# Layer 1's third step: operands kept in SBUF, the bias added by TensorE, VectorE's order tied, the second step's last product first

## The chip, the cores and the metric

The kernel runs on one core of a Trainium2 chip. The metric is the device time of one execution in microseconds (us), from the runs listed below. A profile of one execution gives the time of each instruction on each engine: TensorE (PE), VectorE (DVE), ScalarE (ACT), GpSimd (POOL) and SyncE (SP), whose queue here issues loads. Matrices that a matmul produces lie in PSUM, in banks of 512 fp32 columns; everything else that an engine works on lies in SBUF, and the large arrays in device memory (HBM).

## The reference

Four graph layers run one after the other on 16 graphs of 1024 nodes with 128 features. Each layer's result is added to its input and normalised row by row. The change is in layer 1, which makes three steps of the following kind on an adjacency that was thinned out first; each step's batch normalisation needs the statistics of all 16 graphs.

```python
def _sage(x, adj, Wr, Wx, b, mf):
    deg = jnp.clip(jnp.sum(adj, axis=-1, keepdims=True), 1.0, None)
    agg = jnp.einsum('bij,bjd->bid', adj, x) / deg
    out = agg @ Wr + x @ Wx + b
    nrm = jnp.maximum(jnp.linalg.norm(out, axis=-1, keepdims=True), NORM_EPS)
    return out / nrm * mf[..., None]
...
h1 = _bn(jax.nn.relu(_sage(x, adj_d, Wr1, Wx1, b1, mf)), g1, be1)
h2 = _bn(jax.nn.relu(_sage(h1, adj_d, Wr2, Wx2, b2, mf)), g2, be2)
h3 = _bn(jax.nn.relu(_sage(h2, adj_d, Wr3, Wx3, b3, mf)), g3, be3)
xc = jnp.concatenate([h1, h2, h3], axis=-1) * mf[..., None]
return (xc @ Wl + bl) * mf[..., None]
```

## The kernel before

`fast_kernel` does the work; a general version behind it runs only where a flag says that the inputs are not of the expected kind, which they are here. `B` is 16 graphs (called batches), `N` 1024 nodes, `P` 128 partitions, `NT` 8 blocks of 128 nodes, `H2` two halves of 512 columns.

The thinned adjacency lies in SBUF as `Y[b]`, 8 KB of each partition for a batch, in tiles named `carry_...`. Before layer 1 the tiles of batches 0 to 7 are written to HBM (`dil8_d`) and given up; batches 8 to 15 stay. Every step takes the batches in the order 8 to 15, then 0 to 7.

A step is an object of class `Step`, with `l` 0, 1 or 2. Its parts are generators that `take_turns` runs a piece at a time, so that the code of several batches is interleaved:

- `load(b)` fetches the operands. In step three (`l == 2`) these are `hT` (the batch's features, turned) and `ag` (its aggregation), 512 KB each, from `hT_d[1]` and `ag_d`, by SP's queue.
- `out(b)` multiplies, for each of 8 blocks, `hT` by `Wx` and `ag` by `Wr` (L1410, fp32, two passes of TensorE each) into a PSUM bank for four blocks. VectorE adds the bias row and writes `o` (L1412). ScalarE squares `o` into the bank (L1418), VectorE sums the squares (L1419). Then `power_mhalf` takes the floor on VectorE (L744) and the power -1/2 on GpSimd (L745), VectorE multiplies by the mask (L1422) and makes `n`, the rectified and normalised rows (L1426).
- `keep(b)` turns `n` by eight transposes on TensorE (L759), ScalarE copies them to `nT` (L1435), VectorE takes the statistics of the batch normalisation (L1436), and GpSimd's queue stores `nT` (L1437). In steps one and two it goes on: `n` is split in two parts, the adjacency is widened to fp32 pieces `a`, TensorE multiplies (L1306, 32 matmuls of two passes over the two parts in all, each pass 512 columns), VectorE divides by the degree (L1445) and GpSimd's queue stores `ag` (L1447). That product is what the next step loads.

The normalisation of a step is not applied to its rows. `norm` turns the statistics into a scale and a shift (L1340 to L1345), and `take_norm` puts them into the next step's `Wr` and `Wx` and, by a small matmul `pc` (L1333), into its bias row `brow` (L1334). So step three's weights need all of step two's statistics. The last batch of step two is the exception in the order: its statistics come first (`next(rest)`), and the rest of its `keep`, in the list `left`, is interleaved with the first round of step three.

The order on each engine is not that of the program text: the framework places instructions by estimated times, within what the data and buffers allow. A buffer that is used again waits for its last readers. In PSUM there are four banks of tag `h` (`ps_h`), which `out` and the transposes share, and four of tag `acc` (`ps_a`), which the products of the adjacency use. In SBUF, `nT` of step three has two buffers, `n`, `ag` and `hT` three each.

During step three the memory of layer 2 is opened (`Layers23`), its weights are loaded and scaled (L1207 to L1232, two transposes at L709 and L838), and the inputs of its first batches are loaded (`hb`, `A`, `xn`, L1244 to L1251). Layer 2's first matmuls (`py`, L1568) multiply `hb` by `Wl`; `hb` has one buffer for each of the three steps' results.

Of the kernel before, what the change touches and what calls it, by code (L numbers as in the profile page):

```python
# [22 lines left out]
P = 128  # L23
# [616 lines left out]
def fast_kernel(ctx: ExitStack, tc: tile.TileContext, t: dict, out: bass.AP, flag: bass.AP):  # L640
# [46 lines left out]
    def nat(ap):  # L687
        return ap.rearrange("(t p) d -> p t d", p=P)
# [569 lines left out]
    with ExitStack() as ph:  # L1258
# [39 lines left out]
        def adjacency_product(pieces, parts):  # L1298

            for h in range(H2):  # L1300
# [6 lines left out]
                                             start=(jt == 0 and p == 0), stop=(jt == NT - 1 and p == 1))  # L1307
                yield acc, slice(h * 512, (h + 1) * 512)

        class Step:  # L1310


# [14 lines left out]
            def take_norm(self):  # L1327

                ab = bn_ab[self.l - 1]
                ws = wts.tile([P, P], F32, name="ws")  # L1330
                nc.vector.tensor_add(ws, self.Wr, self.Wx)
                pc = ps_h.tile([P, P], F32, name="pc", tag="h")
                nc.tensor.matmul(pc, ab[:, 1:2].to_broadcast([P, P]), ws, start=True, stop=True)  # L1333
                nc.vector.tensor_add(self.brow, self.brow, pc)  # L1334
                nc.vector.tensor_scalar(self.Wr, self.Wr, ab[:, 0:1], None, op0=OP.mult)
                nc.vector.tensor_scalar(self.Wx, self.Wx, ab[:, 0:1], None, op0=OP.mult)

            def norm(self):
                mv = wts.tile([P, 2], F32, name=f"bmv{self.l}")
# [7 lines left out]
            def load(self, b):  # L1347
# [6 lines left out]
                if self.l == 0:  # L1354
                    st.x = work.tile([P, NT, P], F32, name="n", bufs=3)
                    nc.sync.dma_start(st.x, nat(x1_d[b]))
                else:

                    tag, bufs = ("rdeg", 3) if self.l == 2 else ("hT", 2)
# [41 lines left out]
            def out(self, b):  # L1401

                st = self.batches[b]
                o = work.tile([P, NT, P], F32, name="o", tag="oT")
                banks = []
                for p, _, blocks in halves(ps_h):
                    banks.append(tiles3(p))
                    for i, j in enumerate(blocks):
                        for n, (x, W) in enumerate(((st.hT, self.Wx), (st.ag, self.Wr))):
                            nc.tensor.matmul(p[:, i * P:(i + 1) * P], x[:, j * P:(j + 1) * P], W,  # L1410
                                             start=(n == 0), stop=(n == 1))
                    nc.vector.tensor_add(o[:, blocks[0]:blocks[-1] + 1, :], tiles3(p),  # L1412
                                         self.brow[:, None, :].to_broadcast([P, 4, P]))
                yield
                ss = small.tile([P, NT], F32, name="ss")
                for h, sq in enumerate(banks):
                    k = slice(4 * h, 4 * h + 4)
                    nc.scalar.activation(sq, o[:, k, :], AF.Square)  # L1418
                    nc.vector.tensor_reduce(ss[:, k], sq, AX.X, OP.add)  # L1419
                yield  # L1420
                rn = power_mhalf(small, ss, floor=1e-24, name="rn")
                nc.vector.tensor_mul(rn, rn, mf[:, b * NT:(b + 1) * NT])  # L1422
                st.n = work.tile([P, NT, P], F32, name="n", bufs=3)
                for h in range(H2):
                    k = slice(4 * h, 4 * h + 4)
                    nc.vector.scalar_tensor_tensor(st.n[:, k, :], o[:, k, :], 0.0, half_rows(rn[:, k]),  # L1426
                                                   op0=OP.max, op1=OP.mult)
                yield

            def keep(self, b):  # L1430

                st = self.batches[b]
                nT = work.tile([P, N], F32, name="nT", tag="hi" if self.l == 2 else "oT")
                for p, c, k in turned(ps_h, st.n):
                    nc.scalar.copy(nT[:, c], p)  # L1435
                    nc.vector.bn_stats(self.stats[:, b * H2 + k.start // 4, :], nT[:, c])  # L1436
                nc.gpsimd.dma_start(hT_d[self.l][b], nT)  # L1437
                yield
                if self.l < 2:
                    parts = split(st.n)  # L1440
                    pieces = list(widened(st.A))
                    yield
                    ag = work.tile([P, N], F32, name="ag", bufs=3)
                    for acc, c in adjacency_product(pieces, parts):
                        nc.vector.tensor_mul(ag[:, c], acc, st.rdeg[:, c])  # L1445
                        yield
                    nc.gpsimd.dma_start(ag_d[b], ag)  # L1447
                yield

        before = None  # L1450
# [5 lines left out]
        for l in range(3):  # L1456
            step = Step(l, before)
            if l:
                before.norm()
                step.take_norm()  # L1460
            lead = 0 if l == 1 else 1
            take_turns([step.load(b) for b in order[:1 + lead]])
            if l == 0:
# [2 lines left out]
            for i in range(B + lag[l]):  # L1466
# [2 lines left out]
                    streams.append(step.load(order[i + 1 + lead]))  # L1469
                if l == 0 and i + 1 < B:  # L1470
                    streams.append(step.first(order[i + 1]))
                if i < B:
                    streams.append(outs[i] if l < 2 else islice(outs[i], 1))
                if l == 2 and i:
                    streams.append(outs[i - 1])
                if i > lag[l]:
                    streams.append(step.keep(order[i - 1 - lag[l]]))
                take_turns(streams)
                if l == 2 and i == 0:

# [273 lines left out]
```

## Time and profile before

| what | time |
|---|---|
| median of 3 runs | 2961.86 us |
| lowest and highest run | 2958.01 and 2962.2 us |
| the profiled execution | 2964.0 us |
| its span, first to last instruction | 2962.2 us |
| TensorE busy in the span | 2725.4 us (92%) |
| VectorE busy | 2196.2 us (74%) |
| ScalarE busy | 2024.2 us (68%) |
| GpSimd busy | 325.8 us (11%) |

In the views that follow, a line of a group gives the line of the program, the engine, the operation, the output and input tiles, the shapes and the count; then the busy time in us and the mean of one in ns; then the idle time of the engine just before, with what ended it. In the table by stage each engine has its busy time in us and its count of instructions; `PEclk` is the granted clock of TensorE as a share of the full one, and the DMA share is that of the core's 16 DMA engines. The chain of waits is followed back from the end: each piece has its start, its length and what it was. The timeline has start, length, engine and instruction.

### The profile page before, as it was taken

The page shows a single profiled execution, that of the slowest core. Times are in us where ns is not written, and L with a number is a line of the kernel's source. Part 1 is how long each engine was busy: PE and PEld are TensorE (multiplying, and loading weights), DVE is VectorE, ACT ScalarE, POOL GpSimd, SP SyncE. Part 2 cuts the span into 40 slices and gives each one's busy share as a digit, 9 for nine tenths or more (in the row PEclk, how much of TensorE's full clock was granted, in tenths as well). Part 3 has the DMA queues.
Part 4 walks back from the last instruction along what each step waited for, and adds up shares of the span by engine and source line. Part 5 has one row for each costly group of instructions (what it writes and reads, how often), then busy time and mean ns, then how long its engine had stood idle before and what let it go on. Part 6 is the DMA issues. An engine that isn't in the chain of part 4 may idle for free.

```text
span 2962.2 us, 42088 instructions
## 1 busy us (share of the span) xinstructions
PE 2725.4 (92%) x14771; PEld 1695.2 (57%) x14834; DVE 2196.2 (74%) x6087; ACT 2024.2 (68%) x3476; POOL 325.8 (11%) x295
## 2 busy tenths in 40 slices
PE   7999999996999889999899988999999999999996
PEld 3444444443666657877788873555555555555554
DVE  5777777777999976776688785777777777776765
ACT  6788888874788786666555435666666667676753
POOL 0000000030000001111122230001000101000000
PEclk9999999997999999999999997999999999999998
DMA  5444444420000052233467681111111111111000
GB/s 187 135 157 151 163 163 157 151 91 16 2 2 2 2 195 82 100 107 136 162 212 266 228 327 50 47 62 64 61 68 69 60 58 57 57 57 57 22 15 23
DMA packets 124125, 297.91 MB, mean 101 GB/s; under 512 B 12672, under 2 KB 65664, under 8 KB 116736
## 3 DMA queue, kind: packets, MB, share of 16 engines
q1 hardware_dynamic: 103440, 211.65, 21.6%
q0 software_dynamic: 20464, 83.47, 7.1%
q8 instruction: 119, 1.95, 0.3%
q14 instruction: 102, 0.84, 0.1%
HBM read 211.04 MB, written 84.02 MB: 100 GB/s over the span
## 4 chain that ended last, share of the span: by engine, by line
PE 36%; issue 19%; DVE 17%; POOL 4%; ACT 4%; DMA 2%; SPq 0%; POOLq 0%; DVEq 0%; ACTq 0%
PE ph L1550 8%; PE acc L1306 7%; PE ph L766 5%; PE acc L1626 4%; PE ph L1410 3%; PE pmm L724 3%; POOL ln_rstd L745 2%; PE ph L759 2%; DVE ln_st L794 2%; PE ph L1536 2%; DVE em L1612 2%; ACT xn L801 2%; POOL rn L745 1%; DVE A L1679 1%; PE acc L981 1%
## 5 line engine op out<-in xcount | busy, mean ns | idle before, releaser
L724 PE MATMUL pmm<-G,hT 128*128 128x512 f32 x1024 | 512.8, 614 | 10.7 <-DVE mx L1612 6.7
L801 ACT ACTIVATE xn<-xn,ln_nb,ln_rstd 128x128 f32<-128x128 f32 x512 | 207.4, 481 | 112.9 <-DVE ln_nb L799 112.8
L724 PEld LDWEIGHTS pmm<-G,hT 128*128 128x128 f32 x1024 | 175.0, 193 | 166.7 <-issue 118.3
L745 POOL TENSOR_TENSOR ln_rstd<-ln_rstd,mhalf 128x8 f32<-128x8 f32 (+1 forms) x68 | 115.9, 1704 | 1323.9 <-DVE nmx L1614 606.7
L1306 PE MATMUL acc<-a,lo 128*128 128x512 f32 x768 | 243.5, 401 | 15.5 <-DVE lo L1273 15.5
L1626 PE MATMUL acc<-em,hs 128*128 128x512 f32 x512 | 251.8, 611 | 3.5 <-DVE hs L1623 1.9
L981 PE MATMUL acc<-em,hs 128*128 128x512 f32 x512 | 245.7, 601 | 6.5 <-DVE hs L978 5.6
L1306 PE MATMUL acc<-a,hi 128*128 128x512 f32 x768 | 244.1, 402 | 3.7 <-ACT hi L1272 3.5
L1145 ACT ACTIVATE q<-s,negc 128x512 f16<-128x512 f32 x256 | 170.6, 697 | 59.2 <-DVE negc L1124 22.3
L1143 PE MATMUL s<-step,carry 128*128 128x384 bf16 (+3 forms) x1034 | 199.4, 304 | 7.9 <-DVE carry L1113 3.2
L1157 ACT ACTIVATE carry<-pc,negone 128x512 fp8e4<-128x512 f32 x256 | 166.8, 699 | 38.3 <-PE pc L1156 28.9
L972 DVE CUSTOM_DVE_ANT_0 em<-pmm,msk 128x1024 f32<-128x1024 f32 x128 | 155.9, 1218 | 40.6 <-PE acc L981 20.3
L1306 PEld LDWEIGHTS acc<-a,lo 128*128 128x128 f32 x768 | 144.4, 190 | 54.8 <-DVE lo L1273 21.1
L1612 DVE CUSTOM_DVE_ANT_0 em<-pmm,msk 128x1024 f32<-128x1024 f32 x128 | 155.6, 1216 | 25.9 <-PE acc L1626 21.3
L922 ACT ACTIVATE carry<-an 128x1024 fp8e4<-128x1024 f32 x128 | 134.4, 1050 | 50.7 <-DMA an<-in_adj 50.5
L1306 PEld LDWEIGHTS acc<-a,hi 128*128 128x128 f32 x768 | 143.0, 190 | 37.1 <-ACT hi L1272 4.0
L1607 ACT ACTIVATE msk<-A,nbig 128x1024 bf16<-128x1024 fp8e4 x128 | 145.9, 1140 | 26.6 <-DVE mx L1612 23.4
L974 ACT ACTIVATE em<-em,mx 128x1024 f32<-128x1024 f32 x128 | 146.0, 1141 | 25.4 <-DVE mx L972 22.7
L981 PEld LDWEIGHTS acc<-em,hs 128*128 128x128 f32 x512 | 90.9, 189 | 123.9 <-issue 87.2
L1410 PE MATMUL ph<-Wx,hT 128*128 128x128 f32 x768 | 153.4, 282 | 3.0 <-ACT nT L1435 1.4
L1410 PE MATMUL ph<-Wr,ag 128*128 128x128 f32 x768 | 151.1, 279 | 1.4 <-DMA ag<-ag_d 1.2
L1666 ACT CAST A<-A 128x1024 fp32r<-128x1024 fp8e4 x64 | 64.2, 1040 | 124.8 <-PE ph L1550 124.6
(294 smaller groups left out, 6181.9 us busy)
## 6 DMA issues: line engine op xcount, KB each, us to landing
an<-in_adj SPq DMA_DIRECT2D x128, 512.0 KB, 3.5
adj_d<-carry POOLq DMA_DIRECT2D x16, 1024.0 KB, 4.2
A<-dil_d SPq DMA_DIRECT2D x16, 1024.0 KB, 7.1
rdeg<-rdeg_d SPq DMA_DIRECT2D x32, 512.0 KB, 4.2
ag_d<-ag POOLq DMA_DIRECT2D x32, 512.0 KB, 5.3
ag<-ag_d SPq DMA_DIRECT2D x32, 512.0 KB, 6.3
A<-adj_d SPq DMA_DIRECT2D x16, 1024.0 KB, 4.7
xn<-in_x SPq DMA_DIRECT2D x16, 512.0 KB, 4.2
```

The costliest lines, as they stand in the source:

```text
L724: nc.tensor.matmul(p[:, h * 512:(h + 1) * 512], lhsT, rhs[:, h * 512:(h + 1) * 512], start=True, stop=True)
L745: nc.gpsimd.tensor_tensor(r, r, mhalf[:, :n], op=OP.pow)
L801: nc.scalar.activation(r[:, k.start + i, :], r[:, k.start + i, :], AF.Identity, scale=rstd[:, i:i + 1], bias=nb[:, i:i + 1])
L981: nc.tensor.matmul(s.acc[:, c], hs, em[:, c], start=(jt == 0), stop=(jt == NT - 1))
L1143: nc.tensor.matmul(s[:, lo or 0:], y, twos if lo is None else step[:, :512 - lo], start=(j == 0), stop=(j == len(terms) - 1))
L1145: nc.scalar.activation(q[:, h * 512:(h + 1) * 512], s, AF.Abs, bias=st.negc[:, i:i + 1])
L1157: nc.scalar.activation(Y[b][:, hb, ks], pc, AF.Relu, bias=negone, saturate=False)
L1306: nc.tensor.matmul(acc, part[:, jt, :], pieces[h * NT // 2 + i][:, j, :], start=(jt == 0 and p == 0), stop=(jt == NT - 1 and p == 1))
L1410: nc.tensor.matmul(p[:, i * P:(i + 1) * P], x[:, j * P:(j + 1) * P], W, start=(n == 0), stop=(n == 1))
L1550: nc.tensor.matmul(p, part[:, jt, :], A[:, jt, c], start=(jt == 0 and i == 0), stop=(jt == NT - 1 and i == 1))
L1612: nc.vector.tensor_tensor_reduce(em, e, msk, 1.0, 0.0, op0=OP.add, op1=OP.max, accum_out=mx)
L1626: nc.tensor.matmul(s.acc[:, c], hs, em[:, c], start=(jt == 0), stop=(jt == NT - 1))
```

## The change

Seven things are changed, all in layer 1 and nearly all for step three alone:

1. The batches 0 to 7 get a place in SBUF. `home(b)` is the tile of `Y[b + 8]`, read as fp32: it is exactly two times 1024 columns. Step two's `keep` writes `nT` and `ag` of these batches there. `nT` is still stored to HBM, since layer 2 reads it, but `ag` isn't, and step three's `load` fetches nothing for these batches.
2. Step three takes the batches in the order 8, 0, 9, 1, ..., so that a batch that is loaded and one that is kept alternate.
3. The bias row is split in three bf16 parts (`split_bias`), laid on three groups of 32 partitions, and a matmul of 512 columns by a matrix of twos opens each bank with it. The other matmuls add to the bank. The bias addition of VectorE is gone.
4. The sum stays in PSUM: ScalarE squares the bank into `o`, and the last multiplication reads the bank. The banks are those of `ps_a`.
5. The power is emitted with the squares, one turn earlier, and `keep` stands ahead of `out` in a round.
6. `tc.keep_in_program_order` holds VectorE's first sum of squares, its multiplication after the power and the statistics in the order of the program text against one another.
7. `take_turns(left)` runs the rest of step two's last `keep` before step three's first loads and matmuls.

```diff
+        def home(b):
+            words = Y[b + B // 2].bitcast(F32).rearrange("p t n -> p (t n)")
+            return words[:, :N], words[:, N:]
...
             def take_norm(self):
...
+                if self.l == 2:
+                    self.split_bias()
+
+            def split_bias(self):
+                self.bias3 = wts.tile([P, P], BF16, name="bias3")
+                rest = wts.tile([P, P], F32, name="ws")
+                nc.vector.tensor_scalar(self.bias3, self.brow, 1.0 / 64, None, op0=OP.mult)
+                nc.vector.scalar_tensor_tensor(rest, self.brow, 1.0 / 64, self.bias3, op0=OP.mult, op1=OP.subtract)
+                nc.vector.tensor_copy(self.bias3[:64], rest[:64])
+                nc.vector.tensor_sub(self.bias3[:32], rest[:32], self.bias3[:32])
...
             def load(self, b):
...
+                elif hasattr(st, "home"):
+                    st.hT, st.ag = st.home
                 else:
...
             def out(self, b):
...
-                for p, _, blocks in halves(ps_h):
+                end = self.l == 2
+                for p, _, blocks in halves(ps_a, "acc") if end else halves(ps_h):
                     banks.append(tiles3(p))
+                    if end:
+                        nc.tensor.matmul(tiles3(p), twos[:96, :P], self.bias3[:96, None, :].to_broadcast([96, 4, P]),
+                                         start=True, stop=False)
                     for i, j in enumerate(blocks):
                         for n, (x, W) in enumerate(((st.hT, self.Wx), (st.ag, self.Wr))):
                             nc.tensor.matmul(p[:, i * P:(i + 1) * P], x[:, j * P:(j + 1) * P], W,
-                                             start=(n == 0), stop=(n == 1))
-                    nc.vector.tensor_add(o[:, blocks[0]:blocks[-1] + 1, :], tiles3(p),
-                                         self.brow[:, None, :].to_broadcast([P, 4, P]))
+                                             start=(n == 0 and not end), stop=(n == 1 and (i == 3 or not end)))
+                    if not end:
+                        nc.vector.tensor_add(o[:, blocks[0]:blocks[-1] + 1, :], tiles3(p),
+                                             self.brow[:, None, :].to_broadcast([P, 4, P]))
                 yield
                 ss = small.tile([P, NT], F32, name="ss")
-                for h, sq in enumerate(banks):
+                for h, bank in enumerate(banks):
                     k = slice(4 * h, 4 * h + 4)
-                    nc.scalar.activation(sq, o[:, k, :], AF.Square)
-                    nc.vector.tensor_reduce(ss[:, k], sq, AX.X, OP.add)
+                    x, sq = (bank, o[:, k, :]) if end else (o[:, k, :], bank)
+                    nc.scalar.activation(sq, x, AF.Square)
+                    summed = nc.vector.tensor_reduce(ss[:, k], sq, AX.X, OP.add)
+                    if end and not h:
+                        tc.keep_in_program_order(summed)
+                if end:
+                    rn = power_mhalf(small, ss, floor=1e-24, name="rn")
                 yield
-                rn = power_mhalf(small, ss, floor=1e-24, name="rn")
-                nc.vector.tensor_mul(rn, rn, mf[:, b * NT:(b + 1) * NT])
+                if not end:
+                    rn = power_mhalf(small, ss, floor=1e-24, name="rn")
+                scaled = nc.vector.tensor_mul(rn, rn, mf[:, b * NT:(b + 1) * NT])
+                if end:
+                    tc.keep_in_program_order(scaled)
                 st.n = work.tile([P, NT, P], F32, name="n", bufs=3)
                 for h in range(H2):
                     k = slice(4 * h, 4 * h + 4)
-                    nc.vector.scalar_tensor_tensor(st.n[:, k, :], o[:, k, :], 0.0, half_rows(rn[:, k]),
+                    nc.vector.scalar_tensor_tensor(st.n[:, k, :], banks[h] if end else o[:, k, :], 0.0, half_rows(rn[:, k]),
                                                    op0=OP.max, op1=OP.mult)
...
             def keep(self, b):
                 st = self.batches[b]
-                nT = work.tile([P, N], F32, name="nT", tag="hi" if self.l == 2 else "oT")
+                if self.l == 1 and b < B // 2:
+                    st.home = home(b)
+                    nT = st.home[0]
+                else:
+                    nT = work.tile([P, N], F32, name="nT", tag="hi" if self.l == 2 else "oT")
                 for p, c, k in turned(ps_h, st.n):
                     nc.scalar.copy(nT[:, c], p)
-                    nc.vector.bn_stats(self.stats[:, b * H2 + k.start // 4, :], nT[:, c])
+                    st6 = nc.vector.bn_stats(self.stats[:, b * H2 + k.start // 4, :], nT[:, c])
+                    if self.l == 2:
+                        tc.keep_in_program_order(st6)
...
-                    ag = work.tile([P, N], F32, name="ag", bufs=3)
+                    kept = hasattr(st, "home")
+                    ag = st.home[1] if kept else work.tile([P, N], F32, name="ag", bufs=3)
...
-                    nc.gpsimd.dma_start(ag_d[b], ag)
+                    if not kept:
+                        nc.gpsimd.dma_start(ag_d[b], ag)
...
+            if l == 2:
+                order = [b for pair in zip(order[:B // 2], order[B // 2:]) for b in pair]
+            if l == 2:
+                take_turns(left)
+                left = []
...
+                kept = [step.keep(order[i - 1 - lag[l]])] if i > lag[l] else []
+                if l == 2:
+                    streams += kept
                 if i < B:
-                    streams.append(outs[i] if l < 2 else islice(outs[i], 1))
+                    streams.append(outs[i] if l < 2 else islice(outs[i], 2))
                 if l == 2 and i:
                     streams.append(outs[i - 1])
-                if i > lag[l]:
-                    streams.append(step.keep(order[i - 1 - lag[l]]))
+                if l < 2:
+                    streams += kept
```

## The prediction

> **What bounds the kernel now.** I first asked for the busy time by stage. Step three of layer 1 runs from the matmul `pc` that corrects its bias (1675.79) to the aggregation of its statistics (1784.34), 108.55 us; the other rows are the product of step two before it, the middle of the step, and what follows.
>
> ```profile
> core 0: us, PE busy (x) PEld busy (x) DVE busy (x) ACT busy (x) POOL busy (x), PEclk, DMA share, GB/s
> 1475.00:1675.79 200.79, 195.15 (x1160) 169.52 (x1159) 165.69 (x291) 112.96 (x145) 46.26 (x51) 0.99 0.69 237
> 1675.79:1784.34 108.55, 92.97 (x679) 82.17 (x679) 85.25 (x173) 35.73 (x65) 36.32 (x33) 0.95 0.83 298
> 1718.00:1766.00 48.00, 42.38 (x312) 36.74 (x311) 38.82 (x79) 15.24 (x28) 17.50 (x15) 0.96 1.02 386
> ```
>
> Step two is TensorE's (97% busy), so nothing done for its other engines can pay. In step three no engine is full, but the DMA engines are (share 1.02 in the middle), and VectorE is near it. The groups inside the step say what a batch costs:
>
> ```profile
> L1410 PE MATMUL ph<-Wx,hT 128*128 128x128 f32 x256 | 52.5, 288 | 3.0 <-ACT nT L1435 1.4 <-DVE l2WT L710 1.3
> L745 POOL TENSOR_TENSOR rn<-rn,mhalf 128x8 f32<-128x8 f32 x16 | 26.9, 1681 | 34.6 <-DVE rn L744 34.6
> L1419 DVE TENSOR_REDUCE ss<-ph 128x4 f32<-128x512 f32 x32 | 21.7, 682 | 1.5 <-ACT ph L1418 1.3
> L1412 DVE TENSOR_TENSOR o<-ph,b 128x512 f32<-128x512 f32 x32 | 21.2, 683 | 4.0 <-PE ph L1410 3.6 <-PE ph L759 0.4
> L1426 DVE SCALAR_TENSOR_TENSOR n<-o,rn 128x512 f32<-128x512 f32 x32 | 20.8, 683 | 0.1
> L1436 DVE BATCH_NORM_STATS2 stats<-nT 128x6 f32<-128x512 f32 x32 | 20.6, 681 | 1.9 <-ACT nT L1435 1.7
> ```
>
> VectorE does four kinds of pass twice a batch. They start 0.60 us apart in the timeline, so a batch takes it 8 x 0.60 plus two small ones, about 5.1 us, before any wait for GpSimd's power (1.68 us). Third, the chain of waits, a stretch of it:
>
> ```profile
> 1687.01 6.70 DMA ag<-ag_d
> ...
> 1722.69 1.67 POOL rn L745
> 1724.39 0.17 DVE rn L1422
> 1724.55 0.60 DVE ss L1419
> 1725.15 0.61 DVE n L1426
> 1725.81 0.67 PE ph L759 x4
> ...
> 1731.63 7.83 DMA hb<-h1T_d
> 1739.51 1.13 PE py L1568 x2
> ```
>
> It alternates between loads that come late (6.70 and 7.83 us), the power with VectorE behind it, and TensorE. Where none of these binds, the step already repeats in 4.95 us (first L1410 of successive batches at 1700.10, 1705.05 and 1710.00 in the timeline); the mean is 6.8 (108.55 / 16).
>
> **What the skill says.** (1) "TensorE: Matmul & The Clock Gate", section "What's actually happening": after an idle window of about 3.4 us the array's clock is halved until it has been busy for one. The trace agrees: eight transposes at 1780.99, after 5.34 us of idleness, take 1.97 us instead of 1.04. (2) "VectorE: DVE Perf Modes", "Why PSUM operands drop a tier": fp32 from PSUM runs at the plain rate. Here L1412 reads PSUM in 683 ns and L1426 SBUF in 683 ns, so moving L1426 to PSUM costs nothing. (3) "PSUM — Partial Sum Buffer", "The four PSUM rules": a first matmul clears the bits of its whole bank, which is why one wide bias matmul can open a bank for four blocks. No trace of before shows it. (4) "GPSIMD Engine Reference", "Key points": GpSimd contends with VectorE instructions that have two SBUF inputs. The power took 2.06 us once instead of 1.66, without a cause that I can read; beside it will now stand the statistics, with one input.
>
> **The change, part by part.** I also read the order in which the built instructions stand on each engine; it differs only in step three, its edges, and in tile names of step two.
>
> *Bias on TensorE.* Removed: 32 L1412, 2 x 0.60 = 1.2 us of VectorE a batch. Added: two matmuls of 512 columns a batch. The nearest row is one L1306 pass over 512 columns, 0.233 us apart; the clock-gate page's back-to-back price is about 0.216, as an estimate. I take 0.233; the ends are 0.21 and, with a changeover between types, 0.35. TensorE's batch becomes 32 passes of L1410 (3.57 us, 1762.04 to 1765.61) + 8 transposes (0.89) + 0.47 = 4.93 us. The square now starts at the matmul, one pass earlier. The four small instructions that split the bias stand behind `pc`: about 1 us on VectorE, hidden by the product (below); uncovered it would cost that 1 us.
>
> *VectorE's order.* Per batch: two sums, floor, two statistics while GpSimd works, scale, two products. Its cycle: sums 1.20-1.28, floor to scale 1.95 (1763.62 to 1765.57, the power included), 0.20, products 1.28: 4.7 us, below 4.93. The pinned statistics must be ready within the power. After the matmuls of batch i end (0), the transposes of i-1 end at 0.9 and their two copies (0.59 each) at 1.9, behind the square. The floor is at 1.45, the scale at 3.4, so statistics from 1.6 to 2.9 fit with 0.5 us to spare. Queued behind a late statistic are scale, products, and thereby TensorE's bank.
>
> *Banks.* The banks now stay occupied until the products end: 0.75 + 0.66 to the floor, 2.87 from floor to the next transpose (1778.11 to 1780.98), 4.3 us after the matmuls; the next batch's transposes and matmuls cover 4.93. Two batches of the four banks suffice, with 0.6 us to spare.
>
> *Operands from SBUF.* Removed: 16 loads of 512 KB on SP's queue and 8 `ag_d` stores on POOL's. The places are tiles whose last reader is far past. With 8 MB less to load and the interleaved order, what the step still moves is about 21 MB (6 MB of it layer 2's), near 240 GB/s over 89 us, against 386 above; late loads should vanish. SP's new order puts layer 2's `hb` of batch 0 before three later pairs of loads, but it waits for a store some 25 us old. Bound: one load late by 3 us to nothing; I take nothing.
>
> *The last product first.* Fifteen passes of L1306 (3.50 us) stand before the first L1410 instead of behind it: the same work, two VectorE products with it, no `ag_d` store. It hides the bias split.
>
> *Layer 2's first products.* In before, eight L1568 matmuls (two passes of 0.43 us each) stand within the step and one waits for a load of 7.83 us; now they follow it. They fall beside the aggregation and the load of `hb` for batch 1 (3.46 us at 1790.70, in both). TensorE is at half clock there. I take 0, with ends of -2 and +2.
>
> Sum from `pc`: 0.30 + 3.50 + two batches without transposes 2 x 4.04 = 8.08 + a wait of 0.25 for the first product + 14 x 5.0 (4.93 and 0.07 for semaphores) = 70.0 + two weight transposes 0.5 = 82.6, the last matmul's end. Then 4.3 to the last transposes, and 3.36 from there to the aggregation as before (1780.98 to 1784.34). Together 90.3 against 108.55: 18.3 us less. The profiled execution took 2964.0 (span 2962.2 and 1.8 around it), so it would take 2945.7; it is 2.1 above the median of 2961.86, which gives **2943.6**. What is late next is TensorE itself.
>
> **Rivals.** (A) The tie binds: each step pays a wait where I count spare room, and repeats in 5.5 us as the undisturbed steps of before do at 1762.04 to 1767.60 (5.56). For it: my margins are 0.2 to 0.6 us and any wait on TensorE passes through the loop. Against it: the 5.56 contains the 1.2 us removed. 14 x 0.5 = 7 us back: 2950.6. (B) No measurable change: stores of `nT` hold up its two buffers. A copy must wait for the store of two batches ago: it is issued some 3.5 us after its batch's matmuls and the copy comes at 10.6. Stores landed in 2.9 to 9.0 us, median 6.1, on full DMA engines. At 9.0 throughout, a step gains about 1 us, 14 in all: 2957.6. (C) Slower: the same wait, beyond 9.75 us of landing; then copy, pinned statistics, scale, products and banks run in one ring of two steps, 1.25 + 2 + landing, and the period passes 6.5 us, from which the gain is gone. At 12 us it is 7.6: 14 x 2.6 = 36 back, 18 slower: 2980. Against B and C: less traffic. (D) The change does not do what it says: excluded for the order, which I read; TensorE at half clock for the head would cost 2 us.
>
> **How the numbers follow.** My forecast (gains of 14 to 22) has 0.68; A 0.18; larger gains 0.03; B 0.06; C 0.05. Within 0.2% (5.9 us) is about what a measurement cannot tell from no change. Faster: 0.68 + 0.18 + 0.03 = 0.89; same 0.06; slower 0.05. The range takes A in: 2938 from the lower ends of the bias matmuls and of layer 2's start together with less waiting, 2953 from A with layer 2's start at +2.
>
> **What would show it.** Right: no L1412 in step three, TensorE about 97% busy between `pc` and the last matmul at clock 1.00, batches 4.9 to 5.1 us apart, DMA share well under 0.8, some 90 us from `pc` to the aggregation. Wrong: idle time of TensorE's transposes put to VectorE's product in every batch (A), of ACT's copy put to the `h2T` store (B, C), bias matmuls 0.3 us apart, or a later start of layer 2's attention relative to the aggregation.

## The result and the profile after

The changed kernel takes 2939.69 us, the median of five runs (2936.63 to 2942.92), against 2961.37 of the kernel before in the same comparison (five runs, 2954.01 to 2962.2). The ratio is 0.9931 with an interval of 0.9916 to 0.9946, that is 21.7 us less, with 16 to 25 in the interval. The prediction was 2943.6, and 18.3 us less.

First the busy time by stage, with the same columns as before: step two's product, step three from `pc` to the aggregation, the same only up to the last matmul, and the stretch of it in which the DMA engines are fullest. Lines of the changed file are a little later: L1410 is now L1432, L1418 L1442, L1419 L1443, L1422 L1451, L1426 L1457, L1435 L1470, L1436 L1471, L1437 L1474, L1445 L1483, L1568 L1615; the bias matmul is L1428.

```profile
1475.00:1668.17 193.17, 190.40 (x1141) 165.34 (x1140) 160.48 (x278) 110.73 (x142) 41.40 (x42) 1.00 0.65 222
1668.17:1758.55 90.38, 85.53 (x698) 81.06 (x699) 69.20 (x145) 36.83 (x65) 35.32 (x32) 1.00 0.62 225
1668.17:1751.30 83.13, 81.86 (x675) 78.30 (x676) 63.60 (x135) 33.34 (x59) 32.65 (x29) 1.00 0.65 234
1690.00:1722.00 32.00, 31.25 (x266) 30.09 (x265) 25.78 (x51) 14.03 (x25) 13.37 (x12) 1.00 0.99 362
```

Step three takes 90.38 us instead of 108.55, 18.2 less. Up to its last matmul TensorE is busy 81.86 of 83.13 us (98%), at the full clock. VectorE has fallen from 85.25 to 69.20 us. The DMA engines are full for a third of the step (0.99), and TensorE hardly notices: 31.25 of 32 us.

The groups inside the step (L1432 has three more such lines, one for each pair of operands):

```profile
L745 POOL TENSOR_TENSOR rn<-rn,mhalf 128x8 f32<-128x8 f32 x16 | 26.5, 1658 | 49.2 <-DVE rn L744 49.2
L1432 PE MATMUL ph<-Wx,hT 128*128 128x128 f32 x128 | 24.7, 274 | 0.0
...
L1443 DVE TENSOR_REDUCE ss<-o 128x4 f32<-128x512 f32 x32 | 21.4, 680 | 3.2 <-ACT o L1442 2.6
...
L1457 DVE SCALAR_TENSOR_TENSOR n<-ph,rn 128x512 f32<-128x512 f32 x32 | 20.6, 686 | 1.6
L1471 DVE BATCH_NORM_STATS2 stats<-nT 128x6 f32<-128x512 f32 x32 | 20.6, 682 | 4.4 <-ACT nT L1470 4.4
...
L1470 ACT COPY nT<-ph 128x512 f32<-128x512 f32 x32 | 17.7, 589 | 10.1 <-PE ph L759 4.8 <-DMA h2T_d<-nT 4.2 <-DVE ss L1443 0.8
...
L1428 PE MATMUL ph<-bias,step 96*128 96x512 bf16 x32 | 12.2, 381 | 0.0
```

VectorE's three remaining passes cost what they did (682 to 686 ns; the products now read PSUM, at the same price), and the fourth is gone. L1432 never waits. A bias matmul lasts 381 ns, but the next one starts 0.22 us after it (1711.38 and 1711.60 in the timeline), so two cost a batch 0.44. One thing is new: 4.2 us in which ScalarE's copy waits for a store of `nT`.

The chain of waits is TensorE's for most of the step. A stretch of it:

```profile
1695.58 0.87 PE ph L759 x8
1696.67 1.79 PE ph L1432 x16
1698.46 0.22 PE ph L1428
1698.67 1.79 PE ph L1432 x16
1700.56 1.22 PE ph L759 x8
...
1715.59 0.61 ACT o L1442
1716.21 1.22 PE ph L759 x8
```

Eight transposes, then twice a bias matmul with its 16 passes, then the next batch's transposes. The first bias matmuls of successive batches start at 1681.64, 1686.53, 1691.41 and 1696.29, 4.88 us apart. Twice the transposes take 1.22 instead of 0.87 and come late (at 1700.56 and 1716.21); those two batches are 0.45 and 1.01 us longer.

What TensorE waits for within the step, first in the kernel before, then in the changed one (engine, what waited for what, us in total, times, longest):

```profile
PE ph L759 <- DVE n L1426: 7.9, 5, 5.3
PE ph L1410 <- ACT nT L1435: 1.4, 4, 0.7
...
PE ph L1410 <- DMA ag<-ag_d: 1.2, 1, 1.2
PE py L1568 <- DMA hb<-h1T_d: 1.2, 1, 1.2
```

```profile
PE ph L759 <- DVE n L1457: 4.1, 3, 3.6
PE pc L1338 <- DVE bn_ab L1361: 1.1, 1, 1.1
PE ph L759 <- ACT o L1442: 0.7, 1, 0.7
```

This view corrects the reading of the chain. The two late loads that had 6.70 and 7.83 us on the chain of before kept TensorE idle for 1.2 us each. A piece of the chain is as long as its transfer, not as long as the engine stood.

**Not in step three.** The two profiled executions differ by 26.1 us, 8 more than the step. Of these, 6.2 lie ahead of step two, which the change doesn't touch: the first `pc` stands at 1479.7 and 1473.5, and in all 14 profiles of this study it stood between 1472.4 and 1482.4, and at 1479.3 and 1473.7 in two executions of one and the same version (four buffers, below). Another 1.4 lie in step two (196.1 us from the first `pc` to the second, then 194.7), and 0.2 after the aggregation. Compare medians for the whole and the profiles for the step.

### The profile page after: what moved, and what is told of

It is laid out like the page before. It is cut to its first block, busy times and chain, and to the rows that moved or that the text cites. A ratio compares the mean times of both kernels' runs of the same rounds, so it can differ in the third digit from the quotient of the medians.

```text
span 2936.2 us, 42058 instructions
## 1 busy us (share of the span) xinstructions
PE 2715.8 (92%) x14803; PEld 1690.0 (58%) x14866; DVE 2180.2 (74%) x6059; ACT 2025.2 (69%) x3476; POOL 323.4 (11%) x287
## 4 chain that ended last, share of the span: by engine, by line
PE 40%; issue 20%; DVE 17%; POOL 5%; ACT 4%; DMA 1%; POOLq 0%; DVEq 0%; ACTq 0%; SPq 0%
PE ph L1597 8%; PE acc L1306 7%; PE ph L766 5%; PE acc L1673 4%; PE pmm L724 4%; PE ph L1432 4%; PE ph L759 3%; POOL ln_rstd L745 3%; DVE ln_st L794 2%; PE acc L981 2%; PE ph L1583 2%; DVE em L1659 2%; ACT xn L801 2%; POOL rn L745 1%; DVE A L1726 1%
## 5 line engine op out<-in xcount | busy, mean ns | idle before, releaser
L724 PE MATMUL pmm<-G,hT 128*128 128x512 f32 x1024 | 509.9, 611 | 10.7 <-DVE mx L1659 6.7
L1663 ACT ACTIVATE em<-em,nmx 128x1024 f32<-128x1024 f32 x128 | 145.7, 1138 | 0.0
L969 ACT ACTIVATE msk<-carry,l0nbig 128x1024 bf16<-128x1024 fp8e4 x128 | 144.9, 1137 | 0.0
```

Of the source, the lines that this page charges most:

```text
L724: nc.tensor.matmul(p[:, h * 512:(h + 1) * 512], lhsT, rhs[:, h * 512:(h + 1) * 512], start=True, stop=True)
```

## The experiments

Each run has two numbers: the time from `pc` to the aggregation in its profile, and the median of the whole beside the kernel before on the same chip. The first resolves about 1 us (two executions of one kernel differ by 1.0 and 1.3), the second some 5. What is said of single parts rests on the first, which is one profile for each run.

| run | `pc` to aggregation, us | median, us | before beside it | ratio, interval |
|---|---|---|---|---|
| u1_no_homes | 92.0 | 2942.6 | 2959.9 | 0.9944 (0.9925 to 0.9962) |
| u2_bias_vector | 97.5 | 2944.9 | 2959.9 | 0.9949 (0.9934 to 0.9964) |
| u3_no_tie | 99.2 | 2946.6 | 2959.9 | 0.9959 (0.9944 to 0.9974) |
| u4_no_head | 98.9 | 2949.5 | 2959.9 | 0.9962 (0.9948 to 0.9976) |
| m3_order_only | 101.6 | 2949.6 | 2961.3 | 0.9961 (0.9950 to 0.9972) |
| b1_homes_alone | 103.1 | 2954.2 | 2961.3 | 0.9980 (0.9972 to 0.9988) |
| b2_bias_alone | 110.1 | 2959.4 | 2961.3 | 0.9996 (0.9986 to 1.0006) |
| i1_four_buffers | 89.7 | 2938.3 | 2961.3 | 0.9921 (0.9907 to 0.9935) |
| p1_bias_twice | 96.3 | 2947.4 | 2959.5 | 0.9952 (0.9934 to 0.9969) |
| r_after | 91.6 | 2938.5 | 2959.5 | 0.9922 (0.9904 to 0.9940) |
| i1_again | 89.2 | 2937.8 | 2959.5 | 0.9926 (0.9907 to 0.9945) |
| r_before | 109.6 | 2963.8 | 2958.3 | 1.0009 (0.9989 to 1.0030) |

### Are the two kernels' steps typical?

The kernel before, and the changed kernel, once more.

> The kernel before once more, for a second profile of it. Two questions. Is step three's 108.5 us typical, late loads included? Theory: yes, 105 to 110 us, with at least one load of several us on the chain; rival: 103 or less, so that part of the 18 us was an accident of one execution. And is step two itself 1.4 us longer than in the changed kernel (196.1 against 194.7 us from one pc to the next)? Theory (step two is TensorE's in both, the difference is scatter): between 194.5 and 196.7, nothing to be had from the change; rival: 196 again, a small gain that the stores taken out of step two would explain.

> The changed kernel itself once more, beside the version with four nT buffers, to see which of its waits repeat. Theory: copies wait for h2T_d in the first half of the step again, TensorE loses 1 to 2 us there in one or two batches, pc to the aggregation 90 to 91. Rival (those pauses were an accident of one execution): none of them, 88.8 to 89.3.

Step three of before took 109.6 us, with a load of 8.81 us on its chain, for which TensorE stood 2.2 us. Step two took 194.6 us, about as in the changed kernel (194.7 and 194.6): the 1.4 us above are scatter. The changed kernel took 91.6 us, and again it lost 1.09 and 0.92 us at two batches in the first half, with 5.0 us of copies waiting for `h2T_d`. So the 18 us are the change's, and the two pauses repeat.

### The operands from SBUF undone

```diff
-                if self.l == 1 and b < B // 2:
+                if False:
                     st.home = home(b)
```

> The changed kernel with the operands' part undone: all 16 batches are loaded again and step two stores ag_d for all of them; bias on TensorE, tie, batch order and head stay. Theory (the step's loads were late in the kernel before because the DMA engines were full): 12.6 MB come back, so some 33 MB have to move in about 90 us, 366 GB/s, near the 386 to 430 that the engines reached at their fullest; loads come late again, pc to the aggregation takes 96 to 104 us instead of 90.3, and the time is about 2949 (2945 to 2953). Rival (VectorE alone held the step before; with it eased, the loads keep up): pc to the aggregation 90 to 92 us, time 2940 to 2942, TensorE's idle time in the step not put to loads.

92.0 us: the rival's number, and the theory missed by far. All 16 batches are loaded again, and the engines are as full as they can be (the table by stage, a stretch of 30 us):

```profile
1720.00:1750.00 30.00, 28.51 (x242) 27.35 (x240) 23.19 (x48) 12.95 (x24) 12.86 (x12) 1.00 1.04 413
```

A DMA share of 1.04 at 413 GB/s, more than in the kernel before (386), and TensorE is busy 28.51 of 30 us. Over the step, its waits for operand loads add up to 1.8 us (1.4 for `ag`, 0.4 for `hT`). So full DMA engines were hardly a bound here. A reason that fits, though no run tests it: where nothing disturbs the step, a batch's loads are issued 10.7 us before its first matmul (1694.29 and 1704.95 in the timelines), and they landed in 7.2 and 7.8 us in the median. Beside the rest of the change the 12 MB are worth 0.4 to 1.6 us (against 91.6 and 90.4 for the two profiles of the changed kernel), which is about the limit of what one profile can tell.

### The bias on VectorE again

The bias is not split, VectorE adds it to `o`, and the square and the products read `o` again; the banks stay those of `ps_a`.

```diff
-                    if end:
-                        nc.tensor.matmul(tiles3(p), twos[:96, :P], self.bias3[:96, None, :].to_broadcast([96, 4, P]),
-                                         start=True, stop=False)
...
-                    if not end:
+                    if True:
                         nc.vector.tensor_add(o[:, blocks[0]:blocks[-1] + 1, :], tiles3(p),
                                              self.brow[:, None, :].to_broadcast([P, 4, P]))
```

> The changed kernel with the bias on VectorE again (two more passes of it a batch, two bias matmuls less on TensorE); operands from SBUF, tie, batch order and head stay. Theory (VectorE binds then): its order for a batch is two sums 1.28, one bias pass 0.60, floor 0.2, then two statistics and the other bias pass beside the power 1.95, scale 0.2, two products 1.28, together 5.5 us against the 4.88 of TensorE in the changed kernel; 14 batches by 0.6 give 8.7 us more, pc to the aggregation about 99, time about 2948. Rival (the loads were all of it, VectorE had room): the batch falls to TensorE's 4.45 or stays near 4.9, time 2934 to 2940.

97.5 us, near the theory (99). The transposes of successive batches, in the timeline of TensorE:

```profile
1709.58 1.23 PE L759 MATMUL ph<-identf,n 128*128 128x128 f32 x8 [0.49 <-DVE n L1452]
1715.08 1.23 PE L759 MATMUL ph<-identf,n 128*128 128x128 f32 x8 [0.54 <-DVE n L1452]
1720.58 1.23 PE L759 MATMUL ph<-identf,n 128*128 128x128 f32 x8 [0.49 <-DVE n L1452]
```

A batch takes 5.50 us, as summed, and every batch waits half a microsecond for VectorE's products. VectorE binds, although TensorE has 0.44 us less to do.

### The tie taken away

```diff
                     summed = nc.vector.tensor_reduce(ss[:, k], sq, AX.X, OP.add)
-                    if end and not h:
-                        tc.keep_in_program_order(summed)
...
-                if end:
-                    tc.keep_in_program_order(scaled)
...
-                    if self.l == 2:
-                        tc.keep_in_program_order(st6)
```

> The changed kernel without the three ties; the scheduler then puts one of the two statistics ahead of the floor in most batches, and TensorE's order stays as it is. Theory: that statistic (0.64) stands in VectorE's cycle outside the power, 4.7 + 0.64 = 5.3 us against TensorE's 4.88, and it waits for ScalarE's copy; 14 by 0.45 to 0.7 give 6 to 10 us more: pc to the aggregation 97 to 100, time 2946 to 2949. Rival (VectorE has slack enough, the tie does nothing): time 2939 to 2941 and batches 4.88 apart.

99.2 us, inside the theory's 97 to 100. One batch in VectorE's timeline:

```profile
1707.69 1.27 DVE L1443 TENSOR_REDUCE ss<-o 128x4 f32<-128x512 f32 x2
1708.88 0.68 DVE L1467 BATCH_NORM_STATS2 stats<-nT 128x6 f32<-128x512 f32 x1
1709.48 0.15 DVE L744 TENSOR_SCALAR rn<-ss 128x8 f32<-128x8 f32 x1
1709.54 0.69 DVE L1467 BATCH_NORM_STATS2 stats<-nT 128x6 f32<-128x512 f32 x1
1711.79 0.17 DVE L1449 TENSOR_TENSOR rn<-rn,mf 128x8 f32<-128x8 f32 x1 [1.55 <-POOL rn L745]
```

One statistic stands ahead of the floor; then VectorE is idle for 1.55 us until the power is there. The batch takes 5.57 us (sums at 1707.69 and 1713.26) though VectorE is busy only 66.87 of 99.17 us. Its work is the same as in the changed kernel; only the place of 0.6 us of it differs.

### The head taken away

```diff
-            if l == 2:
-                take_turns(left)
-                left = []
```

> The changed kernel without step two's last product at the head: its 15 passes follow the first two batches' products instead. Theory (the same work in another place): the bias split of about 1 us comes onto the path, and the first batch's power (0.8 us of wait now) runs beside the product, so the two about cancel: pc to the aggregation 89.5 to 91.5, time within 1 us of the changed kernel, 2939 to 2941. Rival (the head carries a part of the gain, by the split or by the freed buffers): 3 us or more, time over 2942.5.

98.9 us, 8.5 more: the miss that taught most. Without the head the scheduler puts all 32 passes of step two's last product behind the first batch of step three. In the kernel before, which has no head either, 17 of the 32 stood ahead of `pc`, where TensorE would else wait for the statistics. TensorE's waits and then its timeline, with that stretch empty:

```profile
PE pc L1338 <- DVE bn_ab L1361: 6.7, 1, 6.7
PE ph L1428 <- DVE bias L1352: 1.5, 1, 1.5
```

```profile
1671.06 0.76 PE L1338 MATMUL pc<-ws,bn_ab 128*128 128x128 f32 x2 [6.65 <-DVE bn_ab L1361]
1673.36 0.58 PE L1428 MATMUL ph<-bias,step 96*128 96x512 bf16 x1 [1.54 <-DVE bias L1352]
1673.74 0.63 PE L1432 MATMUL ph<-Wx,hT 128*128 128x128 f32 x2
...
1677.22 0.39 PE L1432 MATMUL ph<-Wx,hT 128*128 128x128 f32 x2
```

Three costs follow. The 17 passes are now on the path: 17 x 0.233 = 4.0 us. The first bias matmul comes 2.30 us after `pc`, 2.1 more than the 0.2 from `pc` to the product's next passes in the changed kernel. And after 6.65 us of idleness TensorE runs at half clock: 3.64 us from this bias matmul to the next (1677.00) instead of 2.01, 1.6 more. The Trainium skill's "TensorE: Matmul & The Clock Gate", "What's actually happening", says that the clock is halved after an idle window of about 3.4 us; the trace agrees, with a granted clock of 0.52 in this stretch. Together 7.7; the last transposes, at half clock too (1.94 instead of 1.22), add 0.7, which makes 8.4 of the 8.5. Two smaller differences nearly cancel: the third batch no longer waits for the first product (0.8 less), and the pauses are longer (1.0 more).

### The parts alone

The order with tie, batches in turn and head, but operands loaded and bias on VectorE (both diffs above together); then, on the kernel before, the operands in SBUF with the batches in turn:

```diff
+                if self.l == 1 and b < B // 2:
+                    st.home = home(b)
+                    nT = st.home[0]
...
+                    kept = hasattr(st, "home")
+                    ag = st.home[1] if kept else work.tile([P, N], F32, name="ag", bufs=3)
...
+            if l == 2:
+                order = [b for pair in zip(order[:B // 2], order[B // 2:]) for b in pair]
```

and, on the kernel before again, without the operands, the bias on TensorE with the split and the banks that it needs:

```diff
+                    if end:
+                        nc.tensor.matmul(tiles3(p), twos[:96, :P], self.bias3[:96, None, :].to_broadcast([96, 4, P]),
+                                         start=True, stop=False)
...
+                    x, sq = (bank, o[:, k, :]) if end else (o[:, k, :], bank)
```

> The changed kernel with both the operands and the bias undone: what stays is VectorE's order with its tie, the order of the batches and the head. Theory (after the first runs: VectorE's order sets the step, and full DMA engines do not hold it as long as each load is issued early enough): the 5.5 us a batch of the run with the bias on VectorE, and some 1.6 us for the loads; pc to the aggregation 98 to 101 us against 108.5 before and 97.5 with the operands kept, time 2946 to 2949. Rival (the loads and VectorE make it worse together, as in the kernel before): 104 us or more, time 2952 or more.

> The kernel before with one part of the change alone: half the operands kept in SBUF and the batches taken in turn; bias, order of the streams and the end of step two as before. Theory (the late loads of before, 6.70 and 7.83 us on its chain, cost about what they last, but VectorE's 5.5 us a batch then shows): 8 to 10 us of the 18 come, pc to the aggregation 98 to 101, time 2949 to 2952. Rival (the loads were only the last to arrive behind an order that was slow by itself): pc to the aggregation 104 to 108, time 2955 to 2961.

> The kernel before with another part alone: bias on TensorE, everything else as before; the scheduler then puts both statistics ahead of the floor, so that VectorE has nothing to do beside the power. Theory (VectorE's order counts, not its load): two sums 1.28, two statistics 1.28, floor 0.2, power 1.95 uncovered, scale 0.2, two products 1.28 are 6.2 us a batch, more than the 5.5 with the bias passes beside the power; the 1.2 us taken off VectorE bring nothing: pc to the aggregation 106 to 112, time 2957 to 2964, no faster than before. Rival (less work on VectorE shortens the step whatever the order): 100 us or less, time 2952 or less.

The order alone: 101.6, a little above the theory's 98 to 101; the transposes come 5.50 us apart again. The operands alone: 103.1, between the two expectations; TensorE's own waits for loads, 2.4 us before, are gone, and where the other 3 of the 5.4 us come from is not settled. The bias alone: 110.1, no faster than before, with a ratio of 0.9996. VectorE's timeline there:

```profile
1719.33 1.29 DVE L1451 SCALAR_TENSOR_TENSOR n<-ph,rn 128x512 f32<-128x512 f32 x2
1720.54 1.27 DVE L1443 TENSOR_REDUCE ss<-o 128x4 f32<-128x512 f32 x2
1721.72 1.27 DVE L1465 BATCH_NORM_STATS2 stats<-nT 128x6 f32<-128x512 f32 x2
1722.92 0.15 DVE L744 TENSOR_SCALAR rn<-ss 128x8 f32<-128x8 f32 x1
1724.86 0.17 DVE L1447 TENSOR_TENSOR rn<-rn,mf 128x8 f32<-128x8 f32 x1 [1.79 <-POOL rn L745]
```

Products, sums, statistics and floor stand in one row, and then VectorE waits 1.79 us for the power: 5.80 us a batch (products at 1719.33 and 1725.13; I had 6.2). VectorE has 18 us less to do than in the kernel before (67.17 against 85.25), and the step is longer. Part of it is the missing head: here too TensorE stood 6.9 us before `pc` and 1.5 for the split, which cost 8.5 in the run above. That run's cost can't be carried over exactly, so how much of it is the order's is not separated here; what is known is the batch: 5.80 us nearly throughout, where the kernel before repeats in 4.95 in its four undisturbed intervals and takes longer in the others.

So the parts do not add up. Alone, operands, order and bias are worth 5.4, 7.0 and -1.5 us, 10.9 together (and the order of the batches is counted in the first two); in one kernel they are worth 18.2. Taken out one at a time, operands, bias, tie and head cost 1.6, 7.1, 8.8 and 8.5. What the operands are worth depends on the rest: with the bias on VectorE it is 4.1 us (101.6 against 97.5).

One thing leaves the step that no run isolates: most of layer 2's first matmuls. The groups of `py` in the step, before and then after (up to 1759):

```profile
L1568 PE MATMUL py<-hb,Wl 128*128 128x512 f32 x16 | 8.3, 600 | 1.2 <-DMA hb<-h1T_d 1.2
```

```profile
L1615 PE MATMUL py<-hb,Wl 128*128 128x512 f32 x4 | 2.1, 614 | 0.0
```

Three profiles have the step's sums in `ps_h`: the two of the kernel before and the one with the operands alone. In them 16 passes of `py` stand in the step, 12 or all 16 ahead of the step's last matmul. In the eleven profiles with the sums in `ps_a` at most eight stand in it, all behind that matmul. Moved behind the aggregation they cost nothing that shows: from there to the end both kernels take the same (1177.9 and 1177.6 us). In a step that TensorE bounds, 12 passes 0.43 us apart would be 5.2 us, an estimate. So a part of the 18 us, up to about that size, may come from this move. The choice of the banks, like the new order of `keep` and `out` in a round, has no run of its own either.

### What is late now

A probe: each bias matmul issued twice, with the bias halved.

```diff
-                        nc.tensor.matmul(tiles3(p), twos[:96, :P], self.bias3[:96, None, :].to_broadcast([96, 4, P]),
-                                         start=True, stop=False)
+                        for again in range(2):
+                            nc.tensor.matmul(tiles3(p), twos[:96, :P], self.bias3[:96, None, :].to_broadcast([96, 4, P]),
+                                             start=not again, stop=False)
```

> A probe: the changed kernel with each bias matmul issued twice and the bias halved, 32 more passes of 512 columns on TensorE and nothing else. Theory (TensorE is what is late now, at every batch): the trace of the changed kernel shows the next pass 0.22 us after a bias matmul's start, so a batch becomes 4.88 + 0.44 = 5.32 us, and pc to the aggregation grows by 32 x 0.22 = 7.0 us less the two pauses that the longer batch may swallow (up to 1.5): 95.8 to 97.4 us, time 2945 to 2947. Rival (something else, VectorE's loop or the stores, is as late as TensorE): 2 us or less more, pc to the aggregation under 92.5.

96.3 us, within the theory's bounds. Batches start 5.31 us apart (1688.67, 1693.99 and 1699.30), 0.43 more than in the changed kernel: 0.22 a matmul, paid in full. TensorE is what is late now.

### The two pauses

ScalarE's timeline in the changed kernel, at the second pause, and then VectorE's:

```profile
1710.71 0.60 ACT L1442 ACTIVATE o<-ph 128x512 f32<-128x512 f32 x1 [1.41 <-PE ph L1432]
1713.30 1.07 ACT L1470 COPY nT<-ph 128x512 f32<-128x512 f32 x2 [1.99 <-DMA h2T_d<-nT]
```

```profile
1713.92 1.28 DVE L1471 BATCH_NORM_STATS2 stats<-nT 128x6 f32<-128x512 f32 x2 [1.68 <-ACT nT L1470]
1715.12 0.15 DVE L1451 TENSOR_TENSOR rn<-rn,mf 128x8 f32<-128x8 f32 x1
1715.37 1.29 DVE L1457 SCALAR_TENSOR_TENSOR n<-ph,rn 128x512 f32<-128x512 f32 x2
```

The copy waits 1.99 us for the store of two batches before; the tied statistics wait for the copy; the scale, though its power is done at 1713.99, waits behind the statistics; the products follow, and TensorE's transposes come at 1716.21. The chain names ScalarE's square as what released them. The square ended there by chance: what they needed was the product, whose first half (0.69 long) ended just before. (The transposes read `n`, not the square's `o`.) Four buffers take the wait away, and nothing else is edited:

```diff
-                    nT = work.tile([P, N], F32, name="nT", tag="hi" if self.l == 2 else "oT")
+                    nT = work.tile([P, N], F32, name="nT", tag=("hT" if b < B // 2 else "hi") if self.l == 2 else "oT")
```

> The changed kernel with four buffers for nT in step three instead of two (the second pair lies in a tile of step two that is free by then); every instruction stays where it is. Theory (TensorE's two pauses of 0.45 and 1.01 us come from copies that wait for the store of two batches before, while the DMA engines are full): both pauses go, no copy waits for h2T_d any more, pc to the aggregation 88.5 to 89.2 instead of 90.3, time 1 to 2 us less, about 2938. Rival (those copies only came late together with something else, the statistics or ScalarE's order): batches still lose 1 us or more, pc to the aggregation 90.

> The version with four nT buffers once more, beside the changed kernel. Theory: no copy waits for h2T_d, successive batches 4.88 apart from the third to the thirteenth, pc to the aggregation 88.8 to 89.7 by how the last transposes fall against TensorE's clock, 0.5 to 1.5 us less than the changed kernel beside it; in the time of the whole kernel that is within the scatter. Rival: 90 or more.

In both, no copy waits for `h2T_d`, and from the third batch to the thirteenth all are 4.88 us apart. The step took 89.7 and 89.2 us against 90.4 and 91.6. That is the mechanism shown, and a version that is no slower; its medians of 2938.3 and 2937.8 against 2939.7 and 2938.5 are within the scatter, so that it is faster as a whole is not shown.

## Why the prediction was right, and where it was not

Its sum, term by term, in us:

| term | predicted | measured | from |
|---|---|---|---|
| `pc` and 15 passes | 3.80 | 3.80 | 1668.17 to 1671.97 |
| two batches without transposes | 8.08 | 8.03 | 4.02 and 4.01 |
| wait for the first product | 0.25 | 0.77 | 5.65 between the second and third batch, less 4.01 and 0.87 |
| 14 batches | 70.0 | 68.3 | 14 x 4.88 |
| weight transposes of layer 2 | 0.5 | 0.76 | two batches longer by 0.22 and 0.54 |
| pauses | 0 | 1.46 | 0.45 and 1.01 |
| to the last matmul's end | 82.6 | 83.2 | 1751.33 |
| to the last transposes | 4.3 | 4.6 | 1755.94 |
| to the aggregation | 3.36 | 2.61 | 1758.55 |
| sum | 90.3 | 90.4 | |

- **TensorE as the next bound** was right, and so were its batch (4.88 against 4.93 and 0.07 for semaphores, since the bias matmul costs 0.22 and no gap was left) and its full clock. The probe confirms it. The upper end of 0.35 for a bias matmul, with a changeover between types, rested on no measured number, and none of it showed.
- **VectorE's cycle** under 4.9 was right, and that the statistics have to lie beside the power. Rival A's extra wait in each batch didn't come. GpSimd's power took 1658 ns in the mean beside the statistics, against 1681 before, so no contention shows.
- **The banks** held; neither L1428, which opens them, nor L1432 waits.
- **Rival B**, the stores of `nT`, was not to bind and does so twice: 1.5 us, not 14. The margin I gave it rested on stores of 6.1 us in the median; the ones that held a copy up were on full DMA engines, which I had expected to be relieved throughout: their share is 0.62 over the step, but 0.99 from 1690 to 1722, where both pauses lie. The sum had no term for this.
- **The tail** is 0.75 us shorter because the last eight transposes took 1.22 us, where the kernel before had 1.97. That was luck: in the second profile of the changed kernel they took 1.94. This and the shorter batch cancel the pauses and the longer first wait: the sum of 90.3 is closer than its terms.
- **The loads** were misread. That "the DMA engines are" full was true and not a bound: with all loads back the step takes 92.0, and TensorE's own waits for loads in the kernel before were 2.4 us. The forecast did not suffer, since the sum was built on TensorE and not on the bytes.
- **Layer 2's first products** were left out of the step and given a cost of 0 behind it; 0.2 us less were measured from the aggregation to the end. So what their leaving brings the step was in the sum, though not named as a gain.
- **The head** was put down as "the same work" with about 1 us for the bias split. Without it the step is 8.5 us longer. It doesn't gain this against the kernel before; it keeps 17 passes ahead of `pc` that the new order would have moved behind it. What was wrong is the price of leaving the head out. The split alone, uncovered, was to cost 1 us and cost 2.1; and I forgot the 17 passes, and that TensorE would stand idle before `pc` and start at half clock.
- **Whole kernel**: 3 us more came than the step gives (21.7 and, in the second comparison, 20.9, against 18.2 and 17.9). From the aggregation to the end the first pair of profiles differs by 0.2 us, the second by 2.8, and the 14 profiles scatter by 4; where the 3 us lie stays open. The interval of 16 to 25 us holds both.

## What to carry to other kernels

In a loop that crosses engines, count for each engine not its busy time but the ring it closes, the waits in it included, and see what lies beside the longest wait: 0.6 us of work a batch moved to the wrong side of a 1.7 us power cost 9 us here, and 18 us of work taken off the same engine brought nothing while its order and the head were left to the scheduler. When a part is made faster, the scheduler's old placements may go with it, so ask of each gap that was filled by chance what will fill it now. Look also at what leaves the measured stretch, not only at what was changed in it. Here a transfer on the chain and full DMA engines were hints only; the wait of the engine that bounds was the price.

## What the runs showed of the hardware that was not expected

- The same pause of TensorE, 3.58 us before the step's last eight transposes, was followed by the full clock in one execution and by half of it in another. The changed kernel, first profile:

```profile
1755.94 1.22 PE L759 MATMUL ph<-identf,n 128*128 128x128 f32 x8 [3.58 <-DVE n L1457]
```

  and its second profile:

```profile
1759.66 1.94 PE L759 MATMUL ph<-identf,n 128*128 128x128 f32 x8 [3.58 <-DVE n L1457]
```

  The granted clock is 1.00 in the first and 0.50 in the second; the two profiles of the version with four buffers took 1.94 and 1.51 us, at 0.50 and 0.76 in the mean. "TensorE: Matmul & The Clock Gate", "What's actually happening", says that the window of about 3.4 us runs freely, whatever the kernel does. That fits: a pause hardly longer than the window halves the clock or not by where it falls, and 0.7 us of a single execution hang on it.
- DMA engines at a share of 1.04 and 413 GB/s over 30 us, in the version that loads all operands, cost TensorE 1.5 us of idleness at most.
- A bf16 matmul of 96 rows and 512 columns takes 0.22 us from start to start between fp32 ones, with no gap for the change of type.
